# Half tiles with stationary tokens beside whole tiles in a mixture of experts, and set-up operations in written order

## The chip, the cores and the metric

The kernel runs on one core of one Trainium2 chip. The core has a matrix engine (PE, with its weight loads as PEld), a vector engine (DVE), a scalar engine (ACT), a general engine (POOL) and queues that issue DMA transfers, SP's above all. The metric is the time of one execution on the device in microseconds (us). The kernel was run nine times; the median counts. One further execution was taken with a profiler, and all lines of the profile and the trace come from it.

## The reference

The input `x` holds 8 sequences of 256 tokens, each of 256 numbers in float32 (2048 tokens). Four layers follow one another, and each adds its result to its input:

```
x = x + L0(x, cond)         # conditioned RMS norm, attention of 16 heads, SwiGLU of 1024
x = x + L1(x, mask, cond)   # masked attention of 16 heads, RMS norm, modulation by cond
x = x + L2(x)               # FFT filter with one gate per quaternion, two rotations
x = x + L3(x, cond)         # mixture of 8 experts, the best 2 of each token
```

The last layer is the one that the change touches most:

```
gate_w = softmax(rms_norm(x) @ wg_W + wg_b + genre @ gg_W + gg_b)   # 8 values for each token
topk_w, topk_i = top_k(gate_w, 2)
h1 = relu(x @ W1[e] + b1[e])      # 256 -> 512
h2 = relu(h1 @ W2[e] + b2[e])     # 512 -> 512
out = sum over the token's two experts of weight * (h2 @ W3[e] + b3[e])   # 512 -> 256
```

With 2048 tokens and two choices each there are 4096 choices to compute, in groups by expert, whose sizes are only known when the router has run.

## The kernel before

**The layers L0 to L2.** Work goes by sequence ("block", b = 0 to 7). The attention of a block has four pieces, for two groups of heads and two halves of the keys. Each piece makes scores (`s_a`, L949), their exponentials on ACT (`pe_a`, L951) and the products with the values (`o_a`, L962). A list interleaves the attentions of L0 and L1. The function `run` walks that list; after every piece it draws projections and SwiGLU pieces (`pg` and `ph` L1032, `pd` L1045) from a generator, as many as a written number of microseconds calls for (`gaps`). PE executes all of this exactly in the order of the text. `run` also takes `beside`, a table that says which further generator moves one step after which piece. The loop over i = 2 to 6 puts three things there: `last` and `rotated` (rotation and routing of a block, `rotate`) and `placed` (`place_choices`). Before each run of that loop it calls `first_norm(i + 2)` (L874 to L876): sums of squares on ACT, an inverse root in some 12 short DVE operations (L602 to L607), and the scaling `xs_n`, on DVE for blocks 0 and 1 and on POOL later. The end of L0 for a block is `x<-pd,xy` on DVE (L1051), with `xy` from POOL (L1011), then `xs` on POOL (L1053) and the transposition `pt_x` on PE.

**Routing and placing.** `place_choices` runs for every two blocks (one group of 512 tokens). It counts the earlier choices of the same expert with two small matmuls, works out a position for each choice (`posi`, L1196), and POOL writes token number and weight to that position of the table `slots` in memory, by 8 indirect DMAs (L1202).

**The experts.** A tile is 256 choices of one expert, the last one of an expert filled up with dummies. Five tiles are sure to be full after three of the four groups; they (`_s` in names) run between the last attention pieces. Fourteen more (`_a`, the constant `ALWAYS = 14`) run at the end, and the function `table` works out on one partition of DVE, from the counts, which expert and which first position each has. If more were needed, a branch at the very end (`tc.If`) would compute them.

The function `experts` computes the tiles. For tile n, SP loads the records (L1307, token numbers and weights) and the expert's weights (`fetch`, L1313, one transfer of 2.18 MB into one of three buffers in rotation, `WB = 3`), and POOL gathers the tokens (L1320). PE transposes them (`flip`, L1331), and DVE copies them out (`xt`, L1333). `hidden` makes the two layers of 512 with weights as the stationary operand and 256 tokens moving: (2 + 4) x 4 matmuls (L1344), with the relus alternately on ACT (L1352) and DVE (L1354). `give` multiplies by W3 with the tokens stationary (L1367, 8 matmuls), adds the bias (`ye`, DVE L1374), scales (ACT L1375) and adds the rows to the output by an indirect DMA of POOL (L1377). One round n of the loop runs these in PE's order:

```
if n > n0 and n + AHEAD - 1 < n1:
    fetch(n + AHEAD - 1)          # AHEAD = 3: two tiles ahead
    gather(n + AHEAD - 1)
if n < n1:
    yield from hidden(n, ..., "h1")
if n > n0:
    yield from give(n - 1, ...)
if n + 1 < n1:
    flip(n + 1)
    yield
if n < n1:
    yield from hidden(n, ..., "h2")
```

So a tile's output (`give`) is computed within the next tile's round, and its weight buffer comes free there.

**The order of the engines.** PE's instructions stand in written order throughout. Those of DVE do so during the set-up and the first blocks; elsewhere a scheduler decides the order of DVE, ACT, POOL and SP.

Of the kernel before, what the change touches and what calls it, by code (L numbers as in the profile page):

```python
# [16 lines left out]
P = 128  # L17
# [23 lines left out]
NSLOT = 2 * T // SL + E - 1  # L41
# [3 lines left out]
ALWAYS = 14  # L45
# [439 lines left out]
def block_kernel(ctx: ExitStack, tc: tile.TileContext, a: dict, out: bass.AP):  # L485
# [144 lines left out]
    nc.vector.tensor_copy(rank, ranki)  # L630
# [43 lines left out]
    def prepare_condition():  # L674

        nc.vector.tensor_scalar(keyseen, maskT8[:, :, 0], -1.0, 1.0, ALU.mult, ALU.add)

        nc.scalar.activation(tanh_c, condT[0:C, :], AF.Tanh, scale=0.5)
        nc.vector.tensor_scalar(half_c, condT[0:C, :], 0.5, None, ALU.mult)
        nc.vector.scalar_tensor_tensor(silu_c, tanh_c, 1.0, half_c, ALU.add, ALU.mult)  # L680

        for va in va_bufs["a1"]:
            nc.gpsimd.memset(va, 1.0)
            for t in range(NQ):
                nc.gpsimd.tensor_scalar(va[:, t], va[:, t], keyseen[:, t : t + 1], None, ALU.mult)
# [42 lines left out]
    def prepare_router():  # L728
        cond_b = pool_b.tile([C, B, P], F32, tag="hT", bufs=1, name="cond_b")
        nc.vector.tensor_copy(cond_b, condT[0:C, :].unsqueeze(2).to_broadcast([C, B, P]))  # L730

        for k in range(KC):
            nc.vector.tensor_scalar(wgs[:, k, :], wg[:, k, :], rmsw[:, k : k + 1], None, ALU.mult)
        nc.vector.tensor_tensor(gb_b, wgb_b, ggb_b, ALU.add)
        return cond_b
# [133 lines left out]
    def normed(src, name, eng=nc.gpsimd):  # L869
        rstd = rstd_of(src, 1e-6, name)  # L870
        xs = wt("xs", [P, NQ, D], f"xs_{name}", 3)
        for t in range(NQ):
            if eng is nc.scalar:
                nc.scalar.activation(xs[:, t, :], src[:, t, :], AF.Copy, scale=rstd[:, t : t + 1])  # L874
            else:
                eng.tensor_scalar(xs[:, t, :], src[:, t, :], rstd[:, t : t + 1], None, ALU.mult)  # L876
        return xs
# [114 lines left out]
    def first_norm(b):  # L992
        s = state[b]
        s["x"] = xs_in.pop(b)
        s["xs1"] = normed(s["x"], f"n1_{b}", nc.gpsimd if b > 1 else nc.vector)
# [230 lines left out]
    full = iota_row("full", NJ, SL)  # L1226
    tno = iota_row("tno", NSLOT, 1)

# [3 lines left out]
    def table(key, n, n_tiles, op):  # L1232

        pc = ps_m.tile([P, E], F32, tag="m", name=f"pcount_{key}")
        nc.tensor.matmul(pc, ones, seen[:, n, :], start=True, stop=True)
        count = row(f"count_{key}", [E])
        if op is ALU.is_ge:

            nc.vector.tensor_scalar(count, pc[0:1, :], -float(SL), None, ALU.add)
        else:  # L1240
            nc.vector.tensor_copy(count, pc[0:1, :])
        more = row(f"more_{key}", [E, NJ])
        nc.vector.tensor_tensor(
            more, count.unsqueeze(2).to_broadcast([1, E, NJ]), full.unsqueeze(1).to_broadcast([1, E, NJ]), op
        )
        nt = row(f"nt_{key}", [E])
        nc.vector.tensor_reduce(nt, more, AX.X, ALU.add)
        gap = row(f"gap_{key}", [E])
        if op is not ALU.is_ge:
            nc.vector.tensor_tensor(nt, nt, done[:, 0:E], ALU.subtract)  # L1250
        nc.vector.tensor_scalar(gap, nt, -float(SL), float(REGION), ALU.mult, ALU.add)
        if op is not ALU.is_ge:
            step = row("step", [E])
            nc.vector.tensor_tensor(step, done[:, 1:], done[:, 0:E], ALU.subtract)
            nc.vector.scalar_tensor_tensor(gap, step, float(SL), gap, ALU.mult, ALU.add)
        end = row(f"end_{key}", [E])
        nc.vector.tensor_copy(end[:, 0:1], nt[:, 0:1])
        for e in range(1, E):
            nc.vector.tensor_tensor(end[:, e : e + 1], end[:, e - 1 : e], nt[:, e : e + 1], ALU.add)
        past = row(f"past_{key}", [n_tiles, E])  # L1260
        nc.vector.tensor_tensor(
            past, tno[:, 0:n_tiles].unsqueeze(2).to_broadcast([1, n_tiles, E]),
            end.unsqueeze(1).to_broadcast([1, n_tiles, E]), ALU.is_ge,
        )
        te = row(f"te_{key}", [n_tiles])
        nc.vector.tensor_reduce(te, past, AX.X, ALU.add)
        skip = row(f"skip_{key}", [n_tiles, E])
        nc.vector.tensor_tensor(skip, past, gap.unsqueeze(1).to_broadcast([1, n_tiles, E]), ALU.mult)
        start = row(f"start_{key}", [n_tiles])
        nc.vector.tensor_reduce(start, skip, AX.X, ALU.add)  # L1270
        first = row(f"first_{key}", [n_tiles])
        nc.vector.scalar_tensor_tensor(first, tno[:, 0:n_tiles], float(SL), start, ALU.mult, ALU.add)
        if op is not ALU.is_ge:
            nc.vector.scalar_tensor_tensor(
                first, done[:, 0:1].to_broadcast([1, n_tiles]), float(SL), first, ALU.mult, ALU.add
            )
        todo = row(f"todo_{key}", [2, n_tiles], I32)
        nc.vector.tensor_scalar(todo[:, 0, :], te, float(E - 1), None, ALU.min)
        nc.vector.tensor_scalar(todo[:, 1, :], first, float(DUMMY), None, ALU.min)
        return nt, end, todo  # L1280
# [3 lines left out]
    def first_table():  # L1284
        nt, end, todos["sure"] = table("sure", (NG - 1) * NTG, SURE, ALU.is_ge)
# [12 lines left out]
    def experts(n0, n1, todo, pl, key, sure):  # L1298

        st = [dict() for _ in range(n1)]  # L1300

        reach = (NG - 1) * TG if sure else T + SL

        def records(n):
            f = nc.sync.value_load(todo[0:1, 1, n : n + 1], min_val=0, max_val=DUMMY)
            rec = pl.tile("rec", [P, NQ2, 4], f"trec_{key}_{n}", I32)
            nc.sync.dma_start(out=rec, in_=slots[bass.ds(f, SL), :].rearrange("(q p) c -> p q c", p=P))  # L1307
            st[n]["rec"] = rec

        def fetch(n):  # L1310
            e = nc.sync.value_load(todo[0:1, 0, n : n + 1], min_val=0, max_val=E - 1)
            w = pl.weights(f"w_{key}_{n}")
# [3 lines left out]
        def gather(n):  # L1316
            rec = st[n]["rec"]
            xg = pl.tile("xg", [P, NQ2, D], f"xg_{key}_{n}")
            for q in range(NQ2):
# [38 lines left out]
        def give(n, last=False):  # L1358
# [14 lines left out]
            for q in range(NQ2):  # L1373
                nc.vector.tensor_tensor(y[:, q, :], pos[q][:, q, :], w[:, B3O:], ALU.add)  # L1374
                nc.scalar.activation(y[:, q, :], y[:, q, :], AF.Copy, scale=rec.bitcast(F32)[:, q, 1:2])  # L1375
            for q in range(NQ2):
# [6 lines left out]
                adds.append(ad)  # L1383
            yield

        fetch(n0)
        for n in range(n0, min(n0 + 6, n1)):
            records(n)
        for n in range(n0, min(n0 + AHEAD, n1)):
            if not sure and n > n0:  # L1390
                fetch(n)
            gather(n)
        yield
        if sure:
            for n in range(n0 + 1, min(n0 + AHEAD, n1)):
                fetch(n)
        flip(n0)
        yield
        for n in range(n0, n1 + 1):
            if n + 6 < n1:  # L1400
                records(n + 6)
            if n > n0 and n + AHEAD - 1 < n1:
                fetch(n + AHEAD - 1)
                gather(n + AHEAD - 1)
# [7 lines left out]
            if n < n1:  # L1412
                yield from hidden(n, st[n].pop("h1"), MC, W1C, W1C + W2C + W3C + MC, "h2")

# [143 lines left out]

    def at_once(*gens):
# [14 lines left out]
    with tc.manual_schedule(engines={mybir.EngineType.DVE}):  # L1574
# [3 lines left out]
        scales()  # L1578
        keep_busy(4, "pw1")
        g0 = first(0)  # L1580
        next(g0)
        first_norm(1)
# [12 lines left out]
        def second_step():  # L1595
            prepare_quaternions()
            yield
# [12 lines left out]
    for i in range(2, B - 1):  # L1610
        if i + 2 < B:
            first_norm(i + 2)

        placed = at_once(place_choices(i // 2 - 2)) if i in (4, 6) else iter(())
        last, rotated = rotated, rotate(i - 2)
        gaps = [7.6, 5.7, 3.8, 5.7, 8.2, 3.8, 2.5, 3.8] if i + 2 < B else [7.6, 3.8, 1.9, 5.7, 7.6, 1.2, 1.9, 3.8]
        run("bbbbbbbb", others(i - 1), gaps, {0: last, 1: last, 2: last, 3: placed, 6: rotated, 7: rotated})
# [15 lines left out]
    sure = experts(0, SURE, todos["sure"], pl, "s", True)  # L1633
# [29 lines left out]
    nt, end, todo = table("rest", NT, NSLOT - SURE, ALU.is_gt)  # L1663
# [6 lines left out]
    used = row("used", [1], I32)  # L1670
    nc.vector.tensor_copy(used, end[:, E - 1 : E])
    over = row("over", [1])
    nc.vector.tensor_scalar(over, end[:, E - 1 : E], -float(ALWAYS), 0.0, ALU.add, ALU.max)
    rare = row("rare", [1], I32)
    nc.vector.tensor_tensor(rare, over, badf, ALU.add)

    for _ in sure:
# [4 lines left out]
    tiles_used = nc.values_load(used[0:1, 0:1], min_val=0, max_val=NSLOT)  # L1682
    flag = nc.values_load(bad[0:1, 0:1], min_val=0, max_val=N_GOOD)
    either = nc.values_load(rare[0:1, 0:1], min_val=0, max_val=N_GOOD + NSLOT)
    with ExitStack() as stack:
        expert_banks(stack, pl)
        for _ in experts(0, ALWAYS, todo, pl, "a", False):
# [5 lines left out]
    with tc.If(either > 0):  # L1693
        with tc.If(tiles_used > ALWAYS), ExitStack() as stack:
# [3 lines left out]
            with tc.manual_schedule(engines={mybir.EngineType.PE}):  # L1698
                for _ in experts(ALWAYS, NSLOT - SURE, todo, pl, "b", False):
# [81 lines left out]
```

## Time and profile before

| | |
|---|---|
| median of nine runs | 773.21 us (767.77 to 778.25) |
| profiled execution | 769.51 us, its span 767.7 us |
| granted PE clock, mean over the span | 0.986 |
| first matmul of the experts' last stage | at 558.93 us |
| weight fetches | 14 for `w_a` and 5 for `w_s`, 2180 KB each |

The span runs from the first to the last instruction in the trace; 1.8 us of the profiled execution lie outside it. In lines of the timeline the columns are start and duration in us, engine, line, operation, the tile written and the tiles read, and how many instructions of the kind follow one another. What stands in brackets is the engine's idle time before them and what ended it. A float32 matmul shows as two records.

### The profile page before, as it was taken

To read this page: it belongs to the slowest core of one execution; us is meant where nothing else is said; L and a number is where in the kernel's file an instruction comes from. 1 tells how busy PE (TensorE), PEld (TensorE's weight loads), DVE (VectorE), ACT (ScalarE), POOL (GpSimd) and SP (SyncE) were. 2 spreads that over 40 slices of the span, in tenths; PEclk is the share of its full clock that TensorE was granted. 3 is DMA by queue.
4 is the path that set the end of the run, shared out by engine and by line. 5 is a ranking of instruction groups with operands and counts; after the bars stand their busy time and mean duration, and the time that the engine had idled before them with its cause. 6 is when DMAs were issued, how large, how long until landed. Compare 5 with 4: busy or idle time off the path is not lost.

```text
span 767.7 us, 11210 instructions
## 1 busy us (share of the span) xinstructions
PE 730.4 (95%) x4312; PEld 553.8 (72%) x4312; DVE 356.4 (46%) x1112; ACT 255.9 (33%) x410; POOL 183.6 (24%) x218
## 2 busy tenths in 40 slices
PE   7999999999989899988899997999899999999995
PEld 6567676767667567656477765788688888888884
DVE  6457443763773653772755834685122222222221
ACT  3444333443542442542542233331111111112111
POOL 7311200100012300004000063025433424324113
PEclk9999999999999999999899999999999999999998
DMA  9300000000020000010000147064775756756612
GB/s 306 122 15 15 1 13 3 14 15 2 15 69 2 15 1 1 29 41 2 15 1 7 63 127 287 12 221 127 226 202 173 242 163 184 237 156 195 210 16 32
DMA packets 28590, 68.57 MB, mean 89 GB/s; under 512 B 8616, under 2 KB 22960, under 8 KB 26096
## 3 DMA queue, kind: packets, MB, share of 16 engines
q1 hardware_dynamic: 19488, 56.39, 21.7%
q0 software_dynamic: 8736, 11.06, 6.8%
q8 instruction: 36, 0.59, 0.3%
q10 hardware_dynamic: 304, 0.32, 0.1%
q14 instruction: 26, 0.21, 0.1%
HBM read 57.71 MB, written 10.05 MB: 88 GB/s over the span
## 4 chain that ended last, share of the span: by engine, by line
PE 79%; DVE 11%; ACT 4%; another core or an unknown queue 3%; issue 2%; DMA 0%; POOL 0%; POOLq 0%; DVEq 0%; ACTq 0%
PE ph_a L1344 19%; PE s_a L949 8%; PE o_a L962 7%; PE ph_s L1344 7%; PE pe_a L1367 6%; PE ph L1032 6%; PE pg L1032 5%; PE pd L1045 5%; PE pk_a L893 3%; PE pq_a L893 3%; PE pe_s L1367 2%; ACT pe_a L951 2%; PE py L985 2%; PE py L1078 2%
## 5 line engine op out<-in xcount | busy, mean ns | idle before, releaser
L951 ACT ACTIVATE pe_a<-s_a 128x2048 f32<-128x2048 f32 x64 | 119.8, 1872 | 102.0 <-PE s_a L949 91.5
L1344 PE MATMUL ph_a<-h_a,w_a 128*128 128x256 f32 x448 | 99.0, 379 | 0.0
L1344 PEld LDWEIGHTS ph_a<-h_a,w_a 128*128 128x128 f32 x448 | 84.1, 190 | 10.9
L949 PE MATMUL s_a<-qz_a,kT_a 32*128 32x512 f32 x512 | 76.0, 655 | 4.5 <-ACT pe_a L951 3.6
L1354 DVE TENSOR_SCALAR h_a<-ph_a,w_a 128x256 f32<-128x256 f32 x56 | 27.1, 484 | 113.2 <-PE ph_a L1344 113.2
L1352 ACT ACTIVATE h_a<-ph_a,w_a 128x256 f32<-128x256 f32 x56 | 26.6, 475 | 120.7 <-DVE h_a L1354 120.7
L962 PE MATMUL o_a<-pe_a,va 128*32 128x256 f32 x1024 | 64.3, 390 | 0.3 <-issue 0.3
L1032 PE MATMUL pg<-xT_n,gate_wT 128*128 128x256 f32 x256 | 62.0, 385 | 0.8 <-DVE xT_n L883 0.8
L1032 PE MATMUL ph<-xT_n,hid_wT 128*128 128x256 f32 x256 | 61.8, 384 | 0.2 <-DVE sg L1038 0.2
L962 PEld LDWEIGHTS o_a<-pe_a,va 128*32 128x32 f32 x1024 | 30.7, 111 | 42.4 <-issue 26.4
L1045 PE MATMUL pd<-out_wT,hT 128*128 128x256 f32 x256 | 59.3, 384 | 0.4 <-DVE hT L1040 0.4
L1032 PEld LDWEIGHTS ph<-xT_n,hid_wT 128*128 128x128 f32 x256 | 47.8, 190 | 14.5 <-DVE y L1010 4.5
L1032 PEld LDWEIGHTS pg<-xT_n,gate_wT 128*128 128x128 f32 x256 | 47.4, 190 | 13.7 <-issue 4.9
L1377 POOL DMA_INDIRECT out<-ye_a,trec_a x28 | 44.3, 1583 | 53.5 <-ACT ye_a L1375 46.5
L1045 PEld LDWEIGHTS pd<-out_wT,hT 128*128 128x128 f32 x256 | 47.6, 190 | 13.0 <-DVE hT L1040 3.9
L971 DVE STREAM_TRANSPOSE tu_a<-o_a 128x512 f32<-128x512 f32 x32 | 22.9, 716 | 69.9 <-PE o_a L962 55.5
L1344 PE MATMUL ph_a<-xt_a,w_a 128*128 128x256 f32 x224 | 50.7, 379 | 1.0 <-DVE xt_a L1333 1.0
L1202 POOL DMA_INDIRECT slots<-rec,posi x32 | 31.1, 973 | 75.0 <-DVE posi L1196 34.5
L1367 PE MATMUL pe_a<-w_a,h_a 128*128 128x256 f32 x216 | 49.0, 379 | 0.0
L1320 POOL DMA_INDIRECT xg_a<-tokens,trec_a x28 | 27.6, 985 | 85.5 <-PE ptx_a L1331 72.3
L1344 PEld LDWEIGHTS ph_a<-xt_a,w_a 128*128 128x128 f32 x224 | 42.5, 190 | 7.0 <-DVE xt_a L1333 1.2
L1367 PEld LDWEIGHTS pe_a<-w_a,h_a 128*128 128x128 f32 x216 | 40.9, 190 | 5.8 <-ACT h_a L1352 0.2
(266 smaller groups left out, 1001.5 us busy)
## 6 DMA issues: line engine op xcount, KB each, us to landing
w_a<-in_experts SPq DMA_DIRECT2D x14, 2180.0 KB
w_s<-in_experts SPq DMA_DIRECT2D x5, 2180.0 KB
x<-in_x SPq DMA_DIRECT2D x8, 256.0 KB
mod<-mod_rows SPq DMA_DIRECT2D x8, 256.0 KB
tokens<-x SPq DMA_DIRECT2D x4, 512.0 KB
out<-x SPq DMA_DIRECT2D x4, 512.0 KB
gate_wT<-in_gate_wT SPq DMA_DIRECT2D x1, 1024.0 KB
hid_wT<-in_hid_wT SPq DMA_DIRECT2D x1, 1024.0 KB
```

Of the source, the lines that this page charges most:

```text
L893: nc.tensor.matmul(pp[:, c, :], w[:, k, c * P : (c + 1) * P], xT[:, k, :], start=k == 0, stop=k == KC - 1)
L949: nc.tensor.matmul(sc[:, j], kT[r, c, kc * P : (kc + 1) * P], qz[r, c], start=True, stop=True)
L951: nc.scalar.activation(pe, sc, AF.Exp)
L962: nc.tensor.matmul(o[32 * i : 32 * i + 32, qd, :], va[:, kc, 8 * c + 4 * qd + i].rearrange("p a d -> p (a d)"), pe[:, 2 * qd + i // 2, i % ...
L1032: nc.tensor.matmul(ps[:, j, :], w[:, k, o : o + P], yT[:, k, :], start=k == 0, stop=k == KC - 1)
L1045: nc.tensor.matmul(pd[:, t, :], hT[:, c, t * P : (t + 1) * P], out_w[:, c, :], start=c == 0, stop=c == HID // P - 1)
L1202: sc = nc.gpsimd.indirect_dma_start(out=slots, out_offset=bass.IndirectOffsetOnAxis(ap=posi[:, t : t + 1], axis=0), in_=rec[:, t, :], in_o ...
L1320: nc.gpsimd.indirect_dma_start(out=xg[:, q, :], out_offset=None, in_=tokens[0:reach, :], in_offset=bass.IndirectOffsetOnAxis(ap=rec[:, q, ...
L1344: nc.tensor.matmul(ph[:, c - c0, :], w[:, o : o + P], src[:, k, :], start=k == 0, stop=k == n_in - 1)
L1354: nc.vector.tensor_scalar(h[:, c, :], ph[:, c - c0, :], bias, 0.0, ALU.add, ALU.max)
L1367: nc.tensor.matmul(pos[q][:, q, :], h2[:, k, q * P : (q + 1) * P], w[:, o : o + D], start=k == 0, stop=k == MC - 1,)
L1377: ad = nc.gpsimd.indirect_dma_start(out=out[0:reach, :], out_offset=bass.IndirectOffsetOnAxis(ap=rec[:, q, 0:1], axis=0), in_=y[:, q, :], ...
```

## The change

1. **Half tiles.** A remainder of at most 128 choices becomes a half tile. `ALWAYS` goes from 14 to 12, and two halves (`HALVES = 2`) run beside whole tiles 3 and 6 of the last stage (`BESIDE`). A half has one set of 128 tokens, which is the stationary operand of all its matmuls; the weights move, 512 columns at a time. After each of the two hidden layers the result is copied to SBUF by ACT, turned back by four transpositions, and goes through four relus alternately on DVE and ACT. After every piece of the whole tile one piece of the half follows. `table` now counts by halves as well, and `half_table` works out expert and position of each half. Records, fetches and gathers follow the list 0, 1, 2, 3, h3, 4, 5, 6, h6, 7 and so on, three items ahead, with the same three weight buffers.
2. **Into the last stage.** The prologue of the last stage is written ahead of the end of the sure tiles, and its first transposition (`flip`) is issued before the last `give` of the sure tiles.
3. **Set-up.** ACT is in written order there too. The factors of `scales` come after the first block's transposition, with three more filler matmuls (`pw2`). The scaling `xs_n` of blocks 0 and 1 is split between DVE and ACT. Some memsets, iotas and casts move to a later step.
4. **Attention loop.** `first_norm(i + 2)` moves from before the run into `beside`, place 0; `last` goes from places 0, 1, 2 to 1, 2, 3, and `placed` from 3 to 4.

The core of the diff:

```diff
-ALWAYS = 14
+HALF = SL // 2
+NBIG = (2 * T + E * (HALF - 1)) // SL
+ALWAYS = 12
+HALVES = 2
+BESIDE = (3, 6)
...
-        s["xs1"] = normed(s["x"], f"n1_{b}", nc.gpsimd if b > 1 else nc.vector)
+        s["xs1"] = normed(s["x"], f"n1_{b}", nc.gpsimd if b > 1 else (nc.vector, nc.scalar))
...
+        def half(n):
+            w, rec, xg = (st[n].pop(i) for i in ("w", "rec", "xg"))
...
+            for k in range(KC):
+                nc.tensor.transpose(pt[:, k, :], xg[:, 0, k * P : (k + 1) * P], ident)
...
+            nc.vector.tensor_copy(x[:, :, 0:P], pt)
             yield
+            for tag, n_in, off, boff in (
+                ("h1", KC, 0, W1C + W2C + W3C), ("h2", MC, W1C, W1C + W2C + W3C + MC),
+            ):
+                ph = pl.bank("h", [P, M], f"p{tag}_{key}_{name}")
+                for k in range(n_in):
+                    o = off + k * M
+                    nc.tensor.matmul(ph, x[:, k, 0:P], w[:, o : o + M], start=k == 0, stop=k == n_in - 1)
+                    if k % 2:
+                        if k == n_in - 1:
+                            hs = pl.tile("hs", [P, M], f"hs_{tag}_{key}_{name}")
+                            nc.scalar.copy(hs, ph)
+                        yield
+                pt = pl.bank("x", [P, MC, P], f"pt{tag}_{key}_{name}")
+                for c in range(MC):
+                    nc.tensor.transpose(pt[:, c, :], hs[:, c * P : (c + 1) * P], ident)
+                x = pl.tile(tag, [P, MC, SL], f"{tag}_{key}_{name}")
+                for c in range(MC):
+                    bias = w[:, boff + c : boff + c + 1]
+                    if c % 2:
+                        nc.scalar.activation(x[:, c, 0:P], pt[:, c, :], AF.Relu, bias=bias)
+                    else:
+                        nc.vector.tensor_scalar(x[:, c, 0:P], pt[:, c, :], bias, 0.0, ALU.add, ALU.max)
+                yield
...
+            for k in range(MC):
+                o = W1C + W2C + k * D
+                nc.tensor.matmul(po[:, 0, :], x[:, k, 0:P], w[:, o : o + D], start=k == 0, stop=k == MC - 1)
+            out_rows(n, y, [po], rec, w, 1)
+            yield
...
+        for n in range(n0, n1 + 1):
+            at = items.index(n) if n < n1 else len(items)
+            up_to(at + 7, "records", records)
+            for i in range(AHEAD):
+                up_to(at + i + 1, "fetch", fetch)
+                up_to(at + i + 1, "gather", gather)
+            if n == n1 and near_end:
+                next(near_end, None)
+            beside = half(("half", n)) if n in halves else iter(())
+            for _ in tile_(n):
+                yield
+                next(beside, None)
...
-    with tc.manual_schedule(engines={mybir.EngineType.DVE}):
+    with tc.manual_schedule(engines={mybir.EngineType.DVE, mybir.EngineType.Activation}):
         keep_busy(9, "pw0")
         first_norm(0)
         set_up_factors(0)
-        scales()
         keep_busy(4, "pw1")
         g0 = first(0)
         next(g0)
+        keep_busy(3, "pw2")
+        scales()
         first_norm(1)
...
-        if i + 2 < B:
-            first_norm(i + 2)
...
-        run("bbbbbbbb", others(i - 1), gaps, {0: last, 1: last, 2: last, 3: placed, 6: rotated, 7: rotated})
+        run("bbbbbbbb", others(i - 1), gaps, {0: norm, 1: last, 2: last, 3: last, 4: placed, 6: rotated, 7: rotated})
...
+    halves = {n: (todo_h, i) for i, n in enumerate(BESIDE)}
+    others_.append(experts(0, ALWAYS, todo, pl, "a", False, halves))
+    next(others_[0])
     for _ in sure:
         pass
```

`out_rows` is the end of the former `give` as a function of its own, `tile_` the body of the former round, and `norm` is `first_norm(i + 2)` as a generator. In the rare branch, further whole tiles and further halves are computed.

## Prediction

> **What bounds the kernel now.** I read the page's busy line first, then the chain, then the experts' stage in the timeline, the SP queue's waits, and the windows around PE's gaps.
>
> ```profile
> PE 730.4 (95%) x4312; PEld 553.8 (72%) x4312; DVE 356.4 (46%) x1112; ACT 255.9 (33%) x410; POOL 183.6 (24%) x218
> PE 79%; DVE 11%; ACT 4%; another core or an unknown queue 3%; issue 2%; DMA 0%; POOL 0%; POOLq 0%; DVEq 0%; ACTq 0%
> ```
>
> PE is busy for 95% and carries 79% of the chain. So removed PE work counts in full, unless PE then waits. One whole tile of the last stage, in PE's timeline:
>
> ```profile
> 569.84 3.62 PE L1344 MATMUL ph_a<-xt_a,w_a 128*128 128x256 f32 x16
> 573.29 3.62 PE L1367 MATMUL pe_a<-w_a,h_a 128*128 128x256 f32 x16
> 576.75 0.60 PE L1331 MATMUL ptx_a<-ident,xg_a 128*128 128x128 f32 x4
> 577.18 7.07 PE L1344 MATMUL ph_a<-h_a,w_a 128*128 128x256 f32 x32
> 584.09 2.10 PE L1344 MATMUL ph_a<-xt_a,w_a 128*128 128x256 f32 x9
> ```
>
> Start to start, a tile takes 584.09 - 569.84 = 14.25 us without a gap. Sixteen records take 573.29 - 569.84 = 3.45, so 0.216 each; a matmul of 256 columns is two records (0.431). A transpose takes (577.18 - 576.75)/4 = 0.108. Now the weights, in SP's timeline and waits:
>
> ```profile
> 577.91 0.35 SPq L1313 DMA_DIRECT2D w_a<-in_experts  x1
> 592.16 0.34 SPq L1313 DMA_DIRECT2D w_a<-in_experts  x1
> ```
> ```profile
> SPq L1313 <- DVE ye_a L1374: 145.9, 11, 13.8
> ```
>
> A fetch leaves 577.91 - 569.84 = 8.07 us into a tile: it waits for a buffer, which the bias addition `ye` of the tile before frees. In the trace its last packet lands 8.2 to 9.8 us after issue (median 9.26), and about 0.5 passes to the semaphore: 17.8 us after that tile's start. Today it is needed 28.5 after, so 10.7 are spare.
>
> The last view is PE's clock after gaps (columns: length, busy time of PE, PEld, DVE, ACT, POOL, granted clock, DMA share, GB/s):
>
> ```profile
> 366.57:373.40 6.83, 5.38 (x40) 1.90 (x40) 4.76 (x18) 3.75 (x3) 0.00 (x0) 0.50 0.18 41
> 468.97:472.38 3.41, 3.41 (x10) 2.70 (x9) 0.48 (x1) 0.47 (x1) 0.13 (x1) 0.50 0.99 418
> 464.00:469.00 5.00, 1.51 (x7) 1.26 (x8) 2.32 (x5) 0.00 (x0) 2.84 (x3) 1.00 0.59 147
> ```
>
> After PE stood for most of 464 to 469, the clock is 0.50 for 3.41 us, a loss of 1.7. The double window costs 3.4.
>
> **Part 1, whole tiles to halves.** The reference's inputs give the experts 173, 190, 600, 732, 754, 773, 450 and 424 choices. By 256 that is 19 tiles, 5 sure and 14; only 600 and 773 leave remainders up to 128. So 12 whole tiles and 2 halves cover all, and no rare branch follows. Removed: 2 x 14.25 = 28.5. A half has 10 transposes (1.08), 6 matmuls of 512 columns (as two of 256: 6 x 0.863 = 5.18) and 4 of 256 (1.73): 8.0, twice 16.0. **-12.5 us**, all on the path, if nothing waits.
>
> Fetches stay 19, but two items now share one tile's time. Buffers rotate by three over the order 0, 1, 2, 3, h3, 4, 5, 6, h6, 7, 8. Tile 5 takes over tile 3's buffer, free only 8.07 us into tile 4, and tile 8 tile 6's, free 8.07 into tile 7. Each is needed at the next tile's start: 17.8 - 14.25 = 3.5 us of waiting (2.5 to 4.3 over the transfers seen), and behind PE's waiting matmul stands all PE work, in written order. **+7.0.** The tiles beside halves take 14.25 + 8.0 = 22.3, so the fetches for tiles 4 and 7, issued about 10.4 in and landing at 20.2, arrive 2 us early. Those for h3 and h6 land 17.85 after a start and are needed at 14.25 + 3.67 = 17.92: a wait of 0 to 0.5. On SP's queue only tile 6's fetch stands behind tile 5's waiting one, and it has a whole tile more.
>
> Will the clock drop at those two waits? Gaps of 2.8 us (464.96), of 1.99 (216.50) and the pair 2.47 and 2.09 (362.37, 365.93) were each followed by half clock; 1.91, 1.83 and 1.64 were not. A wait of 3.5 is above all of these: one low window each, 2 x 1.7 = **+3.4**. [...]
>
> Inside a half every step hands over: copy, relu, copy, relu, with a piece of the whole tile (four matmuls, 1.73 us) as cover. The evictions last 0.475 (ACT) and 0.484 (DVE) at 256 columns, and ACT waits for DVE between them (120.7 us over 56), so four relus in series are between 1.0 and 2.7 with handovers. Lateness is 0 to 1.0 at each of four such groups; I take little, since half the width is nearer the lower end, and with the waits for h3 and h6 **+1.0** (0 to 5). The two halves' table is some 25 short DVE operations of 0.16 to 0.2: at most 5 us behind a table that ends at 528.1, before a fetch issued at 534.07. Nothing, or up to 1 if DVE's evictions queue behind it.
>
> **Part 2, into the last stage.** The changed order puts the first transposition ahead of the last output of the sure tiles.
>
> ```profile
> 554.56 2.93 PE L1367 MATMUL pe_s<-w_s,h_s 128*128 128x256 f32 x12 [1.83 <-DVE h_s L1354]
> 557.33 0.60 PE L1331 MATMUL ptx_a<-ident,xg_a 128*128 128x128 f32 x4
> 558.93 3.29 PE L1344 MATMUL ph_a<-xt_a,w_a 128*128 128x256 f32 x14 [1.01 <-DVE xt_a L1333]
> ```
>
> The gap of 1.01 goes, and 0.43 of the 1.83 is filled by four transposes: **-1.0** (-1.4 to 0, the records and gathers having been moved up with it).
>
> **Part 3, the set-up.** xs of block 0 leaves DVE for half of its 1.25 us (7.31 to 8.56), and small casts up to 9.56 leave the path to the first projection at 10.16. Three extra filler matmuls, some 0.9 us, stand in PE's wait. **-0.5** (-0.9 to +0.4 if the filler is late). Memsets and iotas on POOL move behind the start, where nothing waits.
>
> **Part 4, the attention loop.** The norm goes into the run, routing one step later, the POOL scatters from place 3 to 4. Eight scatters start every 1.27 us, 10 us in all; behind them stands POOL's addition `xs`.
>
> ```profile
> 364.09 0.69 DVE L1051 SCALAR_TENSOR_TENSOR x<-pd,xy 128x512 f32<-128x512 f32 x1 [6.12 <-remote]
> ```
>
> DVE stood still from 357.97 before this addition, though its product was ready at about 359.5, and it began only after the scatters (352.37 to 362.27). Behind it wait the transposition `pt_x` on PE and the copies of `py` on DVE. PE lost 2.47 and 2.09 and drew the double low window: 8.0 us. In the new order the scatters come after `xs`, before the next `xy`, for which POOL waits longest of all today (134.2 us over 8). If x is no longer caught, 8.0 goes; the burst may catch the projections' copies of the next block instead, as `qz_a` was at 252.81 (a gap of 1.91). Between -10 (the other burst's gap too) and +3; I take half of the 8.0: **-4.0**.
>
> **Sum.** -12.5 + 7.0 + 3.4 + 1.0 - 1.0 - 0.5 - 4.0 = -6.6 us. The profiled execution took 769.5 (span 767.7 and 1.8 outside): 762.9. The median of the nine runs is 773.2, 3.7 above; on it, **766.6**.
>
> **Rivals.** *Gain kept* (0.14): the clock holds through the two waits, or both scatter bursts come free. -6.6 - 3.4 = -10.0, or -6.6 - 6.0 = -12.6, both together -16: 757 to 763. For: part 4 removes the largest gaps. Against: every gap above 2 drew the low clock.
>
> *Even* (0.22): the scatters only catch other operations (0 to +3 in place of -4.0) and the waits lie at their upper ends: -6.6 + 4 to 7 = -2.6 to +0.4: 770.6 to 773.6. For: every POOL burst of before stood beside a gap. Or tile 5's fetch shares the engines with the one right behind it; two fetches issued together around 466 landed 8.0 and some 14 us after issue, one after the other, which speaks against.
>
> *Slower* (0.12): the handovers inside the halves aren't covered. There are ten (five each), and PE's order is fixed, so each stops the whole tile too. The one handover of this kind that shows uncovered, `pe_s` behind `h_s`, cost 1.83, another at 538.16 cost 1.35. Ten at 1.35 are 13.5 in place of my 1.0: +5.9 net, 779. It decides from about 1.15 us each. Against: whole tiles with the same chain show no gap in the last stage, with as much cover.
>
> That the change does not do what it says (remainders left to the rare branch) would show as a thirteenth tile, 14 us; the counts exclude it.
>
> **Chances.** Forecast 0.52, the rest as above. About 0.5% (3.9 us) is what a measurement of this kernel can tell from no change. The forecast's case, -4 to -10, and the kept gain are faster: 0.64 with a little lost at its edge; even, 0.24; slower 0.12. The range reaches into the kept gain, -16, and over the even case, +1.3: 757 to 774.5.
>
> **What would show it.** In the last stage 12 whole tiles, two stretches of about 22 us, and two gaps before L1344's first matmul of tiles 5 and 8, 2.5 to 4.3 us, released by a weight transfer, each with a clock of 0.50 behind it. No gaps around 362 to 368. The forecast is wrong if those waits are missing, if gaps appear inside the halves, or if the scatters draw new low windows.

## The result, and the profile after

The changed kernel is slower: 781.35 us (median of 10 runs, 779.76 to 785.0) against 771.4 us for the kernel before (median of 31). The ratio is 1.0133, with a 95% interval of 1.0106 to 1.0159. The forecast was 766.6, faster by 0.85%. The profiled execution has a span of 778.4 us, 10.7 more than before.

The page after, its busy line and its chain:

```profile
PE 725.9 (93%) x4242; PEld 543.9 (70%) x4242; DVE 354.8 (46%) x1129; ACT 257.6 (33%) x414; POOL 180.5 (23%) x214
PE 75%; DVE 12%; ACT 4%; issue 3%; DMA 3%; another core or an unknown queue 1%; POOL 1%; POOLq 0%; DVEq 0%; ACTq 0%
```

PE does lose work, but its share of the span falls from 95% to 93%: more was added in waits than was taken away. Five landmarks in PE's timeline show where (lengths in us, worked out from starts in the two traces):

| stretch | before | after | difference |
|---|---|---|---|
| start to the `s_a` group at 82.04, after at 90.76 (set-up, first SwiGLU) | 82.0 | 90.8 | +8.7 |
| from there to the `s_a` group at 208.12, after at 216.84 | 126.1 | 126.1 | 0.0 |
| to the `s_a` group at 460.16, after at 467.06 (loop with routing, scatters) | 252.0 | 250.2 | -1.8 |
| to the first `ph_a` of the last stage (558.93, after 569.75) | 98.8 | 102.7 | +3.9 |
| last stage, to the end of its last output matmul | 199.4 | 194.3 | -5.2 |
| from there to the end of the span | 9.4 | 14.4 | +5.0 |

The last stage did what was forecast. PE's timeline and SP's, tile 3 with its half, tile 4, and tiles 5 and 8 (in brackets PE's idle time and what ended it; L1411 is the former L1344):

```profile
609.13 1.89 PE L1411 MATMUL ph_a<-xt_a,w_a 128*128 128x256 f32 x8
...
631.36 3.62 PE L1411 MATMUL ph_a<-xt_a,w_a 128*128 128x256 f32 x16
...
648.37 3.69 PE L1411 MATMUL ph_a<-xt_a,w_a 128*128 128x256 f32 x16 [2.59 <-DMA w_a<-in_experts]
...
702.02 5.37 PE L1411 MATMUL ph_a<-xt_a,w_a 128*128 128x256 f32 x16 [2.68 <-DMA w_a<-in_experts]
```
```profile
639.42 0.88 SPq L1380 DMA_DIRECT2D w_a<-in_experts  x2
```

Tile 3 with h3 takes 631.36 - 609.13 = 22.23, without a gap. The fetch for tile 5 leaves 639.42 - 631.36 = 8.06 into tile 4, and PE waits 2.59 and 2.68 for the weights of tiles 5 and 8. The clock after those two waits, in the windows (granted clock is the third number from the end):

```profile
648.37:651.78 3.41, 3.41 (x16) 3.02 (x17) 0.48 (x1) 0.48 (x1) 0.00 (x0) 1.00 1.01 367
702.02:705.43 3.41, 3.41 (x8) 2.78 (x9) 0.00 (x0) 0.00 (x0) 0.00 (x0) 0.50 1.04 395
```

One of the two drew half clock. The set-up is where the time went, in PE's timeline and in ACT's:

```profile
51.47 1.14 PE L958 MATMUL s_a<-qz_a,kT_a 32*128 32x512 f32 x8 [1.17 <-ACT pe_a L960]
...
81.16 3.48 PE L1041 MATMUL ph<-xT_n,hid_wT 128*128 128x256 f32 x8 [3.18 <-ACT coef L818]
```
```profile
78.79 0.91 ACT L881 ACTIVATE xs_n<-y,rq_y_n 128x256 f32<-128x256 f32 x2 [2.29 <-DVE rq_y_n L613]
79.60 0.40 ACT L866 ACTIVATE junk_n<-x 128x256 f32<-128x256 f32 x1
...
80.54 1.05 ACT L818 COPY coef<-pcoef 128x512 f32<-128x512 f32 x2
81.48 1.89 ACT L960 ACTIVATE pe_a<-s_a 128x2048 f32<-128x2048 f32 x1
```

ACT stands 2.29 us in front of `xs_n`, here the scaling of the second norm (SwiGLU's input), which is always on ACT, because it needs a root that DVE is still working out. The copy `coef`, whose inputs have been ready since about 76, stands behind it, and PE waits 3.18 for the bank that `coef` empties. A half-clock window (80.78 to 84.19, granted clock 0.50) began in the last 0.4 us of that PE gap. In the trace of before, ACT made `coef` first and `xs_n` only 4.85 us later:

```profile
70.62 0.59 ACT L811 COPY coef<-pcoef 128x512 f32<-128x512 f32 x1 [2.18 <-PE pcoef L808]
...
75.47 0.89 ACT L874 ACTIVATE xs_n<-y,rq_y_n 128x256 f32<-128x256 f32 x2
```

PE's two gaps are not all of the 8.7 us. At the score at 44.53 (before: 41.09) 3.4 us are lost already, with one more half-clock window (9.10 to 12.51) and a double one (from 36.40) in place of before's single one (from 35.48).

The end shows in SP's waits, before and then after (total, times, longest, in us):

```profile
SPq L1777 <- PEq L1777: 1.7, 2, 1.1
```
```profile
SPq L1922 <- PEq L1922: 5.7, 2, 5.1
```

Behind that line stands one of POOL's last instructions, a DRAIN, which the trace lists with 1.67 us before and 5.67 after; an INC_SWDGE_SEM ahead of it has 0.59 and 1.57.

### The profile page after: what moved, and what is told of

Same layout as the page of the kernel before. It is cut to its first block, busy times and chain, and to the rows that moved or that the text cites. A ratio compares the mean times of both kernels' runs of the same rounds, so it can differ in the third digit from the quotient of the medians.

```text
span 778.4 us, 11071 instructions
## 1 busy us (share of the span) xinstructions
PE 725.9 (93%) x4242; PEld 543.9 (70%) x4242; DVE 354.8 (46%) x1129; ACT 257.6 (33%) x414; POOL 180.5 (23%) x214
## 3 DMA queue, kind: packets, MB, share of 16 engines
q0 software_dynamic: 8352, 10.54, 6.7%
## 4 chain that ended last, share of the span: by engine, by line
PE 75%; DVE 12%; ACT 4%; issue 3%; DMA 3%; another core or an unknown queue 1%; POOL 1%; POOLq 0%; DVEq 0%; ACTq 0%
PE ph_a L1411 15%; PE s_a L958 8%; PE pd L1054 7%; PE o_a L971 6%; PE ph L1041 6%; PE ph_s L1411 6%; PE pe_a L1434 5%; PE pg L1041 5%; PE pk_a L902 4%; PE pq_a L902 2%; DMA w_a<-in_experts 2%; PE pe_s L1434 2%; PE py L1087 2%; ACT pe_a L960 2%
## 5 line engine op out<-in xcount | busy, mean ns | idle before, releaser
L1411 PE MATMUL ph_a<-h_a,w_a 128*128 128x256 f32 x384 | 85.5, 379 | 0.0
L1411 PEld LDWEIGHTS ph_a<-h_a,w_a 128*128 128x128 f32 x384 | 72.1, 190 | 10.2 <-issue 1.0
L1421 DVE TENSOR_SCALAR h_a<-ph_a,w_a 128x256 f32<-128x256 f32 x48 | 23.2, 484 | 100.6 <-PE ph_a L1411 99.5
L1419 ACT ACTIVATE h_a<-ph_a,w_a 128x256 f32<-128x256 f32 x48 | 22.8, 475 | 106.4 <-DVE h_a L1421 103.6
L1448 POOL DMA_INDIRECT out<-ye_a,trec_a x24 | 38.0, 1583 | 68.4 <-ACT ye_a L1446 63.2
L1411 PE MATMUL ph_a<-xt_a,w_a 128*128 128x256 f32 x192 | 45.6, 391 | 6.2 <-DMA w_a<-in_experts 5.3
L1020 POOL TENSOR_TENSOR xy<-y,x 128x512 f32<-128x512 f32 x8 | 10.2, 1271 | 160.0 <-DVE y L1019 160.0
L1411 PEld LDWEIGHTS ph_a<-xt_a,w_a 128*128 128x128 f32 x192 | 37.3, 197 | 12.7 <-issue 6.0
L1434 PE MATMUL pe_a<-w_a,h_a 128*128 128x256 f32 x184 | 42.1, 379 | 0.0
L1062 POOL TENSOR_TENSOR xs<-x,mod 128x512 f32<-128x512 f32 x8 | 10.1, 1268 | 128.1 <-DVE x L1060 128.1
```

The costliest lines, as they stand in the source:

```text
L1411: nc.tensor.matmul(ph[:, c - c0, :], w[:, o : o + P], src[:, k, :], start=k == 0, stop=k == n_in - 1)
L1421: nc.vector.tensor_scalar(h[:, c, :], ph[:, c - c0, :], bias, 0.0, ALU.add, ALU.max)
L1434: nc.tensor.matmul(pos[q][:, q, :], h2[:, k, q * P : (q + 1) * P], w[:, o : o + D], start=k == 0, stop=k == MC - 1,)
L1448: ad = nc.gpsimd.indirect_dma_start(out=out[0:reach, :], out_offset=bass.IndirectOffsetOnAxis(ap=rec[:, q, 0:1], axis=0), in_=y[:, q, :], ...
```

## The experiments

Each kernel was compared with the kernel before in the same series of runs. That kernel's median differed between series (771.2, 750.5, 769.9 and 751.2 us in their order), so only ratios within a series are used. Theory A: the loss sits in the set-up, in ACT's written order. Theory B: it sits in the halves and the end, and the set-up's delay in the trace is chance.

**The four parts, one by one.**

*Part 3 alone* (the set-up edits of the diff; the rows for the tables keep the shape of before).

> Before with part 3 alone (set-up in written order on ACT too, the split scaling, the later scales, three more fillers, the moved memsets). Theory A, the set-up carries the loss: the trace of after is 8.7 us behind before at the score that follows the first SwiGLU pieces, so this kernel is 6 to 9 us slower, with PE gaps near 51 (ACT pe_a behind xs_n, about 1.2) and 78 (ACT coef behind xs_n, about 3.2). Theory B, that delay is the chance of one profiled execution (its half-clock windows fell badly) and the loss sits in the halves and the end of the program: within 2 us of before.

Measured: 1.0121 (1.0076 to 1.0166). PE gaps of 1.18 at 49.2 and 3.18 at 76.9 appear again. Theory A holds: this part alone is nearly the whole loss.

*Part 1 alone* (the diff without its parts 2, 3 and 4).

> Before with part 1 alone (12 whole tiles and two halves, the new table and item list). Theory A: the last stage is 5 to 6 us shorter than before, as in the trace of after (194.3 us from its first L1344 matmul to its last L1367 record, against 199.4), two waits of about 2.6 us for weights at tiles 5 and 8; if the end of the program is 5 us longer as in after (14.4 against 9.3 us behind the last output matmul), the total is within 2 us of before, if that end was chance, 5 to 6 us faster. Theory B: 5 us slower or more.

Measured: 0.9991 (0.996 to 1.0022), even. In its trace the last stage is 192.0 us, 7.4 shorter, with weight waits of 2.24 and 2.44 and no half clock behind them; the end is 14.2.

*Part 4 alone* (the table of `beside` and the place of `first_norm`).

> Before with part 4 alone (norm, routing and scatters at other places of the run). Theory A: in the trace of after this stretch gained 1.8 us (8.7 behind at its start, 6.9 at its end), so 1 to 3 us faster. The prediction's step said 4. Theory B, the gain needs the shifted set-up ahead of it: no change or slower.

Measured: 1.0023 (0.9988 to 1.0058). No gain. The large gaps near 362 and 366 go, but others of 2.54 (263.4) and 2.93 (379.2) take their place. In the trace of the whole change too, DVE's `tu_a` and `xT_n` come only after the moved scatters, with a gap of PE behind:

```profile
270.15 0.96 POOL L1211 DMA_INDIRECT slots<-rec,posi  x1 [0.31 <-issue]
```
```profile
272.56 0.72 DVE L980 STREAM_TRANSPOSE tu_a<-o_a 128x512 f32<-128x512 f32 x1 [7.34 <-PE pv_a L932]
```
```profile
274.39 1.18 PE L932 MATMUL pv_a<-wv,x2T 128*128 128x264 f32 x4 [2.43 <-DVE xT_n L892]
```

*Part 2 alone* (`near_end`, with before's tiles).

> Before with part 2 alone (the last stage's prologue and first transposition ahead of the last output of the sure tiles). The prediction said -1.0. In the trace of after the stretch from the last scores to the first L1344 matmul of the last stage lost about 4 us, some in gaps of 4.6 and 2.8 with half clock behind them. Theory A, that loss is not this part's: -1 to 0. Theory B, the fetches behind the transposition make every engine wait: +1 to +4.

Measured: 0.9997 (0.997 to 1.0024), nothing. The product of the four ratios, 1.0121 x 0.9991 x 1.0023 x 0.9997 = 1.0132, stands against 1.0133 for the whole change: the parts add up. That it comes this close is partly luck, since each ratio is uncertain by 0.3 to 0.45%.

**What in the set-up.** Before with a single edit:

```diff
-    with tc.manual_schedule(engines={mybir.EngineType.DVE}):
+    with tc.manual_schedule(engines={mybir.EngineType.DVE, mybir.EngineType.Activation}):
```

> Before with one edit: ACT stands in written order during the set-up and the first blocks. Part 3 alone was 1.2% slower (about 9 us). Theory A, the written order of ACT does it: the scaling xs_n waits there for the root on DVE and holds the copy coef, which PE waits for; +5 to +9 us, with a PE gap of about 3.2 near 77 behind ACT coef. Rival: the extra fillers, the later scales and the moved memsets do it: within 2 us of before.

Measured: 1.017 (1.014 to 1.0199). One line makes all of part 3's loss (1.0121, in another series). The converse, the changed kernel with that line taken back:

> The changed kernel with ACT taken out of the written order again; all else stays. Theory A: 5 to 9 us faster than the changed kernel, so within 3 us of before, and no gap behind ACT coef. Rival: as slow as the changed kernel, 1.2 to 1.4% over before.

Measured: 1.002 (1.0 to 1.0039), with no gap behind `coef`. Two experiments then asked how the written order costs it. First the copies `coef` on DVE, in the kernel with ACT's written order alone:

```diff
-            nc.scalar.copy(coef[:, 2 * n : 2 * n + 2], pc)
+            nc.vector.tensor_copy(coef[:, 2 * n : 2 * n + 2], pc)
```

> Before with ACT in written order (1.7% slower by itself), and the two copies coef moved from ACT to DVE. The trace with ACT's written order alone is 8 us behind at the score near 91 us, of which 4.2 came between 77 and 91 (a PE gap of 3.17 behind ACT coef, and a half-clock window behind it). Theory A, PE's wait is the queueing of coef behind xs_n on ACT: that gap goes and 3 to 5 us come back, so about 1.1 to 1.3% slower than before. Rival, DVE is as late as ACT there (it makes the roots that xs_n waits for): the gap stays.

Measured: 1.0149 (1.0104 to 1.0193). Theory A's expectation failed. PE's timeline:

```profile
82.33 3.78 PE L1032 MATMUL ph<-xT_n,hid_wT 128*128 128x256 f32 x8 [5.47 <-DVE coef L811]
```

On DVE the copy keeps its written place, now behind both roots, and the gap grows to 5.47. Taking the copy off ACT doesn't help while it stays written behind work that waits. The second experiment took that work's wait away instead:

```diff
-        s["xs"] = normed(y, f"n2_{b}", nc.scalar)
+        s["xs"] = normed(y, f"n2_{b}", nc.vector if b < 2 else nc.scalar)
```

> Before with ACT in written order, and the scaling xs_n of the second norm of blocks 0 and 1 moved from ACT to DVE, which makes the root it waits for. Theory A, the loss is that ACT stands 2.3 us at each such xs_n with pe_a and coef behind it: the gaps near 49 (1.17) and 78 (3.17) shrink to under 1, the score near 91 us comes 4 to 7 us earlier, and the kernel is 0.3 to 0.9% slower than before in place of 1.7%. Rival, the written position of coef itself (behind two more sums of squares) does it: the gap near 78 stays above 2.

Measured: 1.0047 (1.0023 to 1.0072), from 1.017. The `s_a` group of the first landmark comes 6.3 us earlier than with ACT's written order alone (85.2 against 91.5; 1.15 of it already at the first score). Here `xs_n` no longer stands on ACT, and `coef` runs right behind the sums of squares:

```profile
75.11 0.42 ACT L859 ACTIVATE junk_n<-x 128x256 f32<-128x256 f32 x1
75.43 0.19 ACT L859 ACTIVATION_READ_ACCUMULATOR junk_n<-x 128x1 f32 x1
75.53 1.05 ACT L811 COPY coef<-pcoef 128x512 f32<-128x512 f32 x2
```

The two sums of `junk_n` on `x` are still ahead of it, so the rival (the written position behind those) costs little: the PE gap near 78 is gone. The start of this `s_a` group scatters: 80.7 to 86.6 us in the eleven traces with ACT left to the scheduler, 89.9 to 92.3 in the four others in written order, so that 85.2 is no longer late, and before's 82.0 is on the early side. What is left of the loss, 0.5%, has no shown cause. A candidate is a PE wait of 0.6 to 0.7 us near 36 for `xs_n` from POOL, which is in all five traces with ACT in written order and in none of the other eleven.

**The weight waits.** Part 1 alone, with buffers given out by a list, so that tile 5 takes h3's and tile 8 takes h6's:

```diff
-            n = pl.count % WB
+            n = pl.count % WB if slot is None else slot
...
+SLOTS = (2, 0, 1, 2, 0, 1, 0, 2, 1, 0, 1, 2, 0, 1)
```

> Part 1 alone, with the weight buffers given out in another order: tile 5 takes over the buffer of h3 in place of tile 3's, tile 8 that of h6. The two weight waits of 2.2 to 2.7 us before tiles 5 and 8 should go, with any half-clock window behind them: 4.7 us in the profile and up to 1.7 more for each wait that draws one, so 0.6 to 1.0% faster than before, where part 1 alone was even. Rival, the transfers collide elsewhere: the stage from the first L1344 matmul of the last stage to its end stays near 192.

Measured: 0.9919 (0.9889 to 0.9948). The last stage is 186.9 us, and tile 5 follows tile 4 without a gap (619.87 + 14.25 = 634.12):

```profile
619.87 3.62 PE L1411 MATMUL ph_a<-xt_a,w_a 128*128 128x256 f32 x16
...
634.12 1.89 PE L1411 MATMUL ph_a<-xt_a,w_a 128*128 128x256 f32 x8
```

199.4 - 186.9 = 12.5 us: the PE work taken away, with nothing waiting. The buffers' rotation was the cause of both waits.

**The end.** Part 1 alone without its second loop in the rare branch:

```diff
-                for _ in experts(HALVES, E, todo_h, pl, "c", False):
-                    pass
```

> Part 1 alone without the loop over further halves in the rare branch, which isn't taken with these inputs. In the trace of part 1 alone POOL's DRAIN at the end lasts 5.67 us and its INC_SWDGE_SEM 1.57, before 1.67 and 0.59; the whole end is 14.2 against 9.4 us. Theory A: both lengths go by the DMAs that POOL would issue in the skipped branch (before 4 tiles, with halves 2 tiles and 6 halves): the end falls to 9.4 or less and the kernel is 4 to 6 us faster than part 1 alone. Rival, the halves themselves or the larger program do it: the end stays near 14.

Measured: 1.0002 (0.9982 to 1.0023), DRAIN 5.67 as before the edit, the end 14.0. The skipped branch isn't the cause. What remained was the number of DMAs that POOL issues: 116 in the kernel before, 112 with halves. In the kernel with the swapped buffers, one clearing DMA of the set-up was split into five:

```diff
-        nc.gpsimd.dma_start(out=slots.rearrange("(p j) c -> p j c", p=P), in_=blank)
+        rows_ = TABLE // P // 5
+        for j in range(0, TABLE // P, rows_):
+            nc.gpsimd.dma_start(
+                out=slots.rearrange("(p j) c -> p j c", p=P)[:, j : j + rows_, :], in_=blank[:, j : j + rows_, :]
+            )
```

> Part 1 with the swapped buffers (0.8% faster than before), and one clearing DMA of the set-up split into five, so that POOL issues 116 DMAs as in before and not 112. At the end INC_SWDGE_SEM and DRAIN lasted 0.59 and 1.67 us in all kernels with 116 DMAs and 1.57 and 5.67 in all with 112. Theory A, the length goes by that number: the end falls from 13.8 to about 9.2 us and the kernel is 1.3 to 1.5% faster than before. Rival, the halves or the longer program make the end long: no change, 0.8%.

Measured: 0.9841 (0.9812 to 0.9869), 757.27 us against 769.88. INC_SWDGE_SEM is 0.58, DRAIN 1.63, the end 9.2 us, and SP's wait reads like that of before:

```profile
SPq L1916 <- PEq L1916: 1.6, 2, 1.1
```

In the traces of both kernels the landings of POOL's DMAs count on eight semaphores in turn, 111 to 118: the last of 112 on 118, the last of 116 on 114. Is it the multiple of 8? Before with the same splitting has 120:

> Before with the same splitting: 120 DMAs of POOL. If the end is short because the number is not a multiple of 8 (116 against 112; the DMAs count on eight semaphores in turn), it becomes long here: DRAIN 5.67, and the kernel 0.4 to 0.7% slower than before. If a larger number is what shortens it, DRAIN stays at 1.67 or less and the time is that of before. If the number has no part in it, the same.

Measured: 1.0 (0.9977 to 1.0023), DRAIN 1.91, INC_SWDGE_SEM 0.65, the end 9.3. Not the multiple of 8: 112 is long, 116 and 120 are short. The split also raises the packets of POOL's queue (8352 with 112 DMAs, 8432 with 116 in the kernels with halves), so whether DMAs or packets count is not separated. Why 112 is long stays open.

**Mended versions.** The changed kernel with ACT free, the swapped buffers and 116 DMAs:

> The changed kernel with three edits: ACT out of the written order, the swapped buffers, 116 DMAs of POOL. If the parts add up: with ACT free it was 0.2% over before, the weight waits of 2.2 and 2.4 us each drew a low window there (-8 us), and the end is 4.8 us shorter: 1.3 to 1.7% faster than before.

Measured: 0.9898 (0.9861 to 0.9935), 1.0% faster, less than the 1.3 to 1.7% expected. In its trace the stretch ahead of the last stage (the fourth of the table) takes 101.2 us, against 97.7 in the halves with swapped buffers and 116 DMAs of the same series. And the same without part 4:

> The changed kernel without ACT's written order and without part 4, with the swapped buffers and 116 DMAs of POOL. With part 4 it was 1.0% faster than before, the halves with buffers and DMAs alone 1.6%. If part 4 costs the difference (alone it was +0.2%, from -0.1 to +0.6): 1.4 to 1.8% faster. If the moved prologue or the rest of part 3 cost it: 1.0% as before.

Measured: 0.9871 (0.9827 to 0.9915). Its interval overlaps the one with part 4 and the one of the halves alone with buffers and DMAs, so whether part 4 takes something back isn't settled. The best ratio is that of part 1 with the swapped buffers and the split DMA, 1.6% faster than before; it beats both kernels of this case.

## Why the prediction was wrong, point by point

**Part 1, PE work.** Right. A tile with its half takes 22.23 us against 14.25 + 8.0 forecast, and the stage without waits is 12.5 us shorter.

**Part 1, the weight waits.** Right in mechanism, place and cure; the size was 2.59 and 2.68 (2.0 to 2.7 in all traces with the old rotation), not 3.5. They lie at the lower end of the stated bounds (2.5 to 4.3), some below it. The term: 5.3 in place of 7.0.

**Part 1, the clock.** Half right. Eight such waits were seen in four traces (changed kernel, part 1 alone, ACT free, no second loop): four drew one low window, four none. In the changed kernel the term was 1.7 in place of 3.4. The step took every gap above 2 us to draw a window and passed over where the gap falls. Within a trace the low windows start whole multiples of 3.413 us apart (changed kernel: 473.31, 565.47 and 702.00, which are 27 and 40 times 3.413 apart; before: 219.80, 366.57 and 468.97, 43 and 30 times). If each of the four traces is cut into stretches on this grid, the four waits that drew put 2.01, 2.05, 2.22 and 2.66 us of idle time into the one stretch before the window, the other four at most 1.61, 1.63, 1.67 and 2.01 into any one. In the changed kernel the wait of 2.59 lay across two stretches (1.61 and 0.98) and drew nothing, while that of 2.68 had 2.66 in one and drew a window; before's gap of 1.99 at 216.50 lay in a single stretch and drew one too. No limit is shown by this: 2.01 stands on both sides, and before's low window at 35.48 followed a stretch with only 0.12 us of idle time, most of it filled with matmuls of 8 columns.

**Part 1, inside the halves.** Right to its lower end: no gap in either half. The slower rival, ten uncovered handovers, did not happen.

**Part 2.** Forecast -1.0, measured nothing (0.9997). The gap before the first `ph_a`, 1.01 before, stayed with 0.89 (0.90 in part 2 alone), released by the last output matmul in place of the copy.

**Part 3 is the step that failed.** The forecast was -0.5 (-0.9 to +0.4); the part alone costs 1.2%, some 9 us. The step priced what moves out of the path in the first 10 us and passed over the one part of the change that acts on all the first 90: ACT in written order. The order of ACT's instructions was in the trace of before, in which `coef` (70.62) and `pe_a` (42.88) run while `xs_n` waits. The question put to every added wait, what is queued behind it on its engine, was not put to an order that makes waits.

**Part 4.** Forecast -4.0, measured +0.2% (-0.1% to +0.6%). The even rival's step was right: the scatters only catch other operations, `tu_a` and `xT_n` in place of `x`. That the loop's -1.8 us in the table is this part's gain is not shown: in the trace of part 4 alone the same stretch takes 258.1, 6.0 longer than in before.

**The end** had no term. That the change issues fewer POOL DMAs was not looked at; at 112 the DRAIN at the program's end took 4.0 us longer and INC_SWDGE_SEM 1.0.

The stretches of the two traces add up to the longer span: the set-up +8.7, the last stage -5.2, the end +5.0, the loop -1.8, and +3.9 ahead of the last stage, in gaps of 4.61 (470.65) and 2.76 (561.56) with half clock from 473.31 and 565.47, where before had 2.80 (half clock from 468.97) and 1.83 (none). The last stays without a shown cause: part 2 alone shows no loss, and parts 3 and 4 alone, which leave part 2 out, have gaps of 3.60 and 3.15 in place of the 2.76.

## What to carry to other kernels

When an engine's order changes from a scheduler's to the written one, list the instructions on it that wait longest, and what the written order puts behind each: two scalings in front of which ACT stood 2.3 us each cost 1.2% of this kernel (1.017, and 1.0047 with both on DVE). When an item of work becomes shorter, look at each resource in rotation with it: two items in one tile's time made a buffer late that had 10.7 us to spare, and handing the short item's buffer on brought the full 12.5 us. Undo or apply the parts of a change one at a time, since a part that gains can hide one that loses.

## What the runs showed of the hardware

The time from POOL's last DMA instruction to the end of the span was 11.4 us in the changed kernel, with 112 DMAs issued by POOL, and 6.4 in before, with 116. POOL's DRAIN in it took 5.67 us in all five traces with 112, and 1.63 to 1.91 in all eleven with 116 or 120.

DVE's wait beside the burst of indirect DMAs differed between traces of the same loop: `x<-pd,xy` came after 6.12 us of idle time in before (364.09, the last scatter ending at 362.27), and after 3.48, ended by its product `pd`, with ACT's written order alone (366.22). The loop stretch of the table takes 238.2 to 241.5 us in all six traces of the second and fourth series, where the kernel before took 750.5 and 751.2, and 250.2 to 258.1 in the ten other traces. Part 1 alone has a PE gap of 2.42 near 360 in the first series; without its second loop, which isn't executed, it has none above 1.0 there in the second. What differed between the series was not found; the first two ran on the same chip.
